# Two fused attention layers: denominators by 32x32 transposes and one product, seven split steps, and seven moved steps

## The chip, the cores and the metric

The kernel runs on one core of one Trainium2 chip. A core has five engines that run their own instruction streams side by side and wait for each other by semaphores: TensorE (PE, matrix products; its weight loads are listed as PEld), VectorE (DVE), ScalarE (ACT), GpSimd (POOL) and SyncE (SP, which here only issues DMA transfers). The metric is the device time of one execution in microseconds (us); lower is better.

## The reference

Input and output are four images of 64 x 64 positions, that is 4096 tokens, with 256 channels each. Two self-attention layers follow each other on every image (biases left out below where they are added in the plain way):

```python
# layer 1 (l = 0 in the kernel): queries and keys of 32 channels, values of 256
q, k, v = x @ Wq + bq, x @ Wk + bk, x @ Wv + bv
energy = jnp.einsum('bnd,bmd->bnm', q, k)           # 4096 x 4096 per image
x = gamma * jnp.einsum('bnm,bmc->bnc', softmax(energy), v) + x
# layer 2 (l = 1): queries g and keys f of 32 channels, values of 128
f, g, v = x @ Wf + bf, x @ Wg + bg, x @ Wh + bh
beta = softmax(jnp.einsum('bqd,bkd->bqk', g, f))
x = x + jnp.einsum('bqk,bkd->bqd', beta, v) @ Wo + bo
```

A softmax needs, for each query, the exponential of its 4096 scores and the sum of these exponentials, its denominator.

## The kernel before

The images are worked on one after the other. In each image layer 1 runs over 16 blocks of 256 queries and layer 2 over 8 blocks `j` of 512 queries. A block of layer 2 has 16 steps `i`; each step is one `Step` and covers 256 keys. Within a step TensorE makes the scores, keys on the partitions and queries along the row (L532), ScalarE takes the exponential `p` of all 128 x 1024 of them (L544), and TensorE multiplies `p` with the values and adds up in PSUM over the steps (L600). The scores of step `i + 2` are issued ahead of the products of step `i`. They go to two PSUM buffers in turn, called "st" and "pair", each of which is free again when ScalarE has read the scores that are in it.

**Two forms of a step.** A whole step multiplies `p` in fp32. A split step (every step of layer 1, in layer 2 those of `SPLIT1`) takes a second exponential `high` (L542) scaled down by a constant bias; VectorE makes `low` = p - high (L555) and `d`, a correction (L560), and TensorE runs three fp32r products, of `high`, `low` and `d`, with values that are cut in the same way. High and low of a step are issued together, d one step later. Layer 2 has six split steps and ten whole ones per block before the change. `V1` counts the whole steps, and with it go the number of value tiles, the number of early x tiles (`LEAD`) and of the start's side tiles (`LEAD_BUFS`).

**The denominators of layer 2.** All `p` of a block are added up. VectorE adds those of the "kept" steps into `p_sum` (L571, L573). The steps in `MOVED_SUMS` are added by DMA on GpSimd's queue: the `p` of the first one is copied to a tile of tag "e" (L548), that of each further one is added to it by an accumulating DMA (L550). There is one "e" tile, so each of these DMAs waits until the one before has landed. At the block's end VectorE adds the last products to `o` (L657), the moved sums to `p_sum` (L659) and both halves of `p_sum` to `sums` (L660). The four units `output(t)` run within the next block, at its steps 1 to 4: TensorE multiplies `o` by Wo (L667) and, for 128 queries at a time, `sums` by a column of ones (L668), which sums over the partitions and leaves the denominators one per partition; VectorE takes the reciprocal (L670), ScalarE scales with it (L673), and a DMA on GpSimd's queue adds `y` to the output (L675).

**Buffers.** `wide` (L267) gives 128 x 1024 tiles by tag: three of "p" (whole steps), two each of "t" (`high` and `p` of split steps) and "l" (`low` and `d`), one of "d" (`p_sum`) and one of "e". A tile is written again only when all of its readers are done, a DMA that reads it included. `small` (L510) gives four 128 x 256 tiles for layer 1's residual (x_res, x1) and layer 2's `y`.

**Order of work.** The Python loop at L735 writes one order of instructions; each engine runs its part of it strictly in that order. `plan` (L702) places smaller units of work at fixed steps: the ends of the block before at steps 1 to 4, and, for the next layer or image, units of transposes (L392 on VectorE, by 32 x 32 squares), of the q and k projection (L418 to L442, whose result goes to DRAM by L446) and of the value projection (L460). In layer 2 of the first three images these units prepare the next image; the fourth image has none. Loads of q and k (L493) and the accumulating DMAs stand on GpSimd's queue, which also runs the additions L639 and L751; x_res (L750), x1 (L632), the residual output (L640), qk_dram (L446) and the transposed loads (L280) stand on SyncE's.

**The q and k projection.** Its PSUM buffer is one of two side buffers. ScalarE copies the lower half to an SBUF tile "qk" (L439), VectorE adds the upper half and the bias to it (L440), and from that tile the upper part is cast (L441) and the rest found by a subtraction (L442).

**The end.** After the last block the kernel tests all denominators and the largest values against bounds (L807 to L822); where a bound is broken, a general path computes everything anew. It isn't taken with these inputs.

Of the kernel before, what the change touches and what calls it, by code (L numbers as in the profile page):

```python
# [50 lines left out]
F32 = mybir.dt.float32  # L51
# [16 lines left out]
SPLIT1 = (0, 3, 5, 8, 11, 13)  # L68
MOVED_SUMS = (0, 4, 7, 9, 12)
# [169 lines left out]
def fast_path(ctx: ExitStack, tc: tile.TileContext, x, w0, w1, wo, bo, gamma, out, off):  # L239
# [70 lines left out]

    inverse = const.tile([P, 2, B * N // P], F32, name="inverse")
# [12 lines left out]
    for l, (q_w, q_b, k_w, k_b, v_w, v_b) in enumerate((w0, w1)):  # L324
        queue = (nc.scalar, nc.gpsimd)[l]
        w_sb = work.tile([P, NCC, 2 * D], F32, tag="small", bufs=4, name=f"wqk_whole{l}")
# [33 lines left out]
    def bias_units():  # L360


        def issue():
            nc.vector.tensor_scalar(bv, bv, gamma_sb, None, ALU.mult)
            wide_bias = work.tile([P, P], F32, tag="small", bufs=4, name="wide_bias")
# [10 lines left out]
    q_t, moved_sums, first_p, waiting = {}, {}, [], {}  # L376
# [35 lines left out]
    def project_units(b, l, h):  # L412
# [5 lines left out]
        def qk_unit():  # L418
# [10 lines left out]
            whole = data.tile([2 * D, QB0], F32, tag="qk", name=f"qk_{b}_{l}_{h}")  # L429
# [9 lines left out]
            nc.scalar.copy(whole, ps[bottom, :])  # L439
            nc.vector.scalar_tensor_tensor(whole, ps[top, :], bqk[l], whole, ALU.add, ALU.add)  # L440
# [69 lines left out]
    def small(name):  # L510
        return work.tile([P, C], F32, tag="small", bufs=4, name=name)


    class Step:
# [8 lines left out]
        def scores(self):  # L523
# [19 lines left out]
            self.p = wide("t" if self.split and l == 1 else "p", f"p_{self.key}")  # L543
            nc.scalar.activation(self.p, s_flat, AF.Exp)  # L544
            if l == 1 and i in MOVED_SUMS:
                if i == MOVED_SUMS[0]:
                    moved_sums[b, j] = wide("e", f"p_sum_moved_{b}_{j}")
                    nc.gpsimd.dma_start(moved_sums[b, j], self.p)  # L548
                else:
                    nc.gpsimd.dma_start(moved_sums[b, j], self.p, accum_op=ALU.add)  # L550
# [13 lines left out]
        def add_up(self, p_sum):  # L564
# [3 lines left out]
            if self.i == kept[0]:  # L568
                first_p.append(self.p)
            elif self.i == kept[1]:  # L570
                nc.vector.tensor_add(p_sum, first_p.pop(0), self.p)  # L571
            else:
                nc.vector.tensor_add(p_sum, p_sum, self.p)  # L573
# [299 lines left out]
```

## Time and profile before

| | before |
|---|---|
| time, median of 3 runs | 3157.56 us (3156.2 to 3158.73) |
| the profiled execution's own time | 3155.92 us |
| its span in the trace | 3154.1 us |
| mean granted TensorE clock | 0.998 of full speed |
| busy: TensorE / VectorE / ScalarE / GpSimd | 99 / 85 / 68 / 29 % |
| accumulating DMAs of the moved sums (L550), copies (L548) | 128, 32; 512 KB each |
| L668 (denominators), L667 (output projection) | 256, 256 matmul records |

The busy time of an engine is the time in which it has at least one instruction at work, as a share of the span. Matmuls overlap each other in the pipeline, so the price of one is better read from the distance between the starts of two than from its own duration. One statement of the source, such as a fp32 product of 128 x 512, can show up as several records. For a DMA the trace has the issuing instruction on the queue's engine and the landing of the data.

### The profile page before, as it was taken

What the parts mean: (1) busy time and instruction counts of PE and PEld (TensorE: products, weight loads), DVE (VectorE), ACT (ScalarE), POOL (GpSimd) and SP (SyncE); (2) the same over time, 40 slices, a digit from 0 to 9 for tenths busy, and PEclk for the clock granted to TensorE, in tenths of its full rate; (3) what the DMA queues carried; (4) which work ended last, traced back from release to release, by engine and by line L of the source; (5) the groups of instructions that cost most, each with busy time, mean ns of one, the idle gap of its engine ahead of it and who ended that gap; (6) DMA issues with size and microseconds to landing.
All of it is one profiled execution on the core that took longest, in us unless ns stands there. A gap on an engine that the chain in (4) does not pass through costs nothing.

```text
span 3154.1 us, 54090 instructions
## 1 busy us (share of the span) xinstructions
PE 3116.3 (99%) x19908; PEld 2672.0 (85%) x19908; DVE 2689.1 (85%) x3237; ACT 2140.1 (68%) x2835; POOL 900.7 (29%) x1108
## 2 busy tenths in 40 slices
PE   8999999999999999999999999999999999999997
PEld 7999998666799999866679999976668999996664
DVE  7888888888888888888888888898888888888876
ACT  7666666777666666777766666677776666666674
POOL 5232224222422222422242222232223222233221
PEclk9999999999999999999999999999999999999999
DMA  4121114555512121555541112255554111125454
GB/s 119 43 53 47 48 48 104 107 108 105 104 44 51 41 53 47 113 101 112 107 93 47 49 45 51 51 116 107 105 113 81 48 46 47 49 65 105 97 95 73
DMA packets 391392, 239.49 MB, mean 76 GB/s; under 512 B 266672, under 2 KB 355248, under 8 KB 391120
## 3 DMA queue, kind: packets, MB, share of 16 engines
q0 software_dynamic: 68160, 134.86, 22.0%
q1 hardware_dynamic: 322048, 100.76, 13.4%
q8 instruction: 161, 2.64, 0.4%
q14 instruction: 111, 0.91, 0.1%
q10 hardware_dynamic: 912, 0.33, 0.1%
HBM read 82.58 MB, written 67.11 MB: 47 GB/s over the span
## 4 chain that ended last, share of the span: by engine, by line
PE 91%; DVE 3%; DMA 2%; issue 2%; ACT 1%; POOL 0%; SPq 0%; DVEq 0%; ACTq 0%; POOLq 0%
PE acc L600 24%; PE acc L582 23%; PE acc_pair L582 23%; PE st L532 14%; PE psv L464 4%; PE psqk L422 2%; PE pso L667 2%; DVE d L560 1%; DVE low L555 1%; ACT p L544 1%; DVE p_sum L573 1%; DMA p_sum_moved<-p 0%; DMA squares<-in_x 0%; PE pso L668 0%; DMA squares<-x_dram 0%
## 5 line engine op out<-in xcount | busy, mean ns | idle before, releaser
L542 ACT ACTIVATE high<-st,down 128x1024 fp32r<-128x1024 f32 x704 | 786.5, 1117 | 703.2 <-PE st L532 362.8
L544 ACT ACTIVATE p<-st 128x1024 f32<-128x1024 f32 x1024 | 1042.5, 1021 | 166.3 <-PE st L532 143.8
L560 DVE SCALAR_TENSOR_TENSOR d<-low,high 128x1024 fp32r<-128x1024 f32 x704 | 871.0, 1237 | 227.0 <-PE acc_pair L582 223.7
L555 DVE TENSOR_TENSOR low<-p,high 128x1024 fp32r<-128x1024 f32 x704 | 936.6, 1330 | 142.6 <-ACT p L544 141.6
L532 PE MATMUL st<-q,k 128*128 128x256 f32 (+1 forms) x3072 | 706.3, 338 | 2.5 <-DMA k<-qk_parts 1.4
L600 PE MATMUL acc<-p,v 128*128 128x512 f32 x1280 | 611.0, 597 | 0.0
L532 PEld LDWEIGHTS st<-q,k 128*128 128x128 f32 x3072 | 470.0, 189 | 103.3 <-issue 40.6
L639 POOL TENSOR_TENSOR x_res<-x,bo 128x256 f32<-128x256 f32 x128 | 212.5, 1660 | 879.3 <-DVE x L628 879.2
L600 PEld LDWEIGHTS acc<-p,v 128*128 128x128 f32 x1280 | 233.1, 189 | 161.8 <-issue 143.4
L573 DVE TENSOR_TENSOR p_sum<-p_sum,p 128x1024 f32<-128x1024 f32 x288 | 352.6, 1224 | 9.4 <-ACT p L544 5.8
L582 PE MATMUL acc<-v0h,high 128*128 128x258 f32 x2048 | 341.6, 284 | 1.2 <-ACT high L542 1.2
L582 PE MATMUL acc<-v0d,d 128*128 128x258 f32 x2048 | 339.2, 287 | 2.6 <-DVE d L560 2.2
L582 PE MATMUL acc<-v0l,low 128*128 128x256 f32 (+1 forms) x2048 | 329.3, 283 | 0.6 <-DVE low L555 0.5
L582 PE MATMUL acc_pair<-v0h,high 128*128 128x258 f32 x2048 | 329.8, 283 | 0.0
L582 PE MATMUL acc_pair<-v0l,low 128*128 128x256 f32 (+1 forms) x2048 | 328.8, 282 | 0.0
L582 PE MATMUL acc_pair<-v0d,d 128*128 128x258 f32 x2048 | 328.5, 282 | 0.0
L582 PEld LDWEIGHTS acc<-v0h,high 128*128 128x128 f32 x2048 | 286.0, 189 | 3.1 <-issue 1.4
L582 PEld LDWEIGHTS acc<-v0d,d 128*128 128x128 f32 x2048 | 281.5, 190 | 5.6 <-DVE d L560 4.9
L582 PEld LDWEIGHTS acc<-v0l,low 128*128 128x128 f32 x2048 | 282.2, 190 | 1.8 <-DVE low L555 1.3
L582 PEld LDWEIGHTS acc_pair<-v0h,high 128*128 128x128 f32 x2048 | 282.1, 189 | 0.0
L582 PEld LDWEIGHTS acc_pair<-v0l,low 128*128 128x128 f32 x2048 | 281.1, 189 | 0.0
L582 PEld LDWEIGHTS acc_pair<-v0d,d 128*128 128x128 f32 x2048 | 281.0, 189 | 0.0
(108 smaller groups left out, 3332.5 us busy)
## 6 DMA issues: line engine op xcount, KB each, us to landing
p_sum_moved<-p POOLq DMA_DIRECT2D x160, 512.0 KB, 4.7
x_res<-in_x SPq DMA_DIRECT2D x128, 128.0 KB, 2.1
qk_dram<-qk_parts SPq DMA_DIRECT2D x128, 128.0 KB, 1.9
x_dram<-x SPq DMA_DIRECT2D x128, 128.0 KB, 1.7
out<-x_res SPq DMA_DIRECT2D x128, 128.0 KB, 1.7
squares<-x_dram SPq DMA_DIRECT2D x512, 32.0 KB, 1.9
out<-y POOLq DMA_DIRECT2D x128, 128.0 KB, 3.2
q<-qk_dram POOLq DMA_DIRECT2D x252, 64.0 KB, 2.2
```

The lines of the kernel that those rows point to most:

```text
L422: nc.tensor.matmul(ps, wqk[l][:, c, :], x_parts[key][n][:, c, :], start=(c == n == 0), stop=(c == NCC - 1 and n == 1),)
L464: nc.tensor.matmul(ps[:, t, :], xT[key][:, c, t * P : (t + 1) * P], wv[l][:, c, :], start=(c == 0), stop=(c == NCC - 1),)
L532: nc.tensor.matmul(st[:, g, :], k_t[b, l, kt // NT][:, kt % NT * P : (kt % NT + 1) * P], q_t[b, l, j * n // QB][:, q0 : q0 + n], start=Tru ...
L542: nc.scalar.activation(self.high, s_flat, AF.Exp, bias=down)
L544: nc.scalar.activation(self.p, s_flat, AF.Exp)
L555: nc.vector.tensor_sub(self.low, self.p, self.high.bitcast(F32))
L560: nc.vector.scalar_tensor_tensor(self.d, self.low.bitcast(F32), -UP, self.high.bitcast(F32), ALU.mult, ALU.add)
L573: nc.vector.tensor_add(p_sum, p_sum, self.p)
L582: nc.tensor.matmul(acc[2 * s + which][:, :width], p[:, g * QB0 + s * P : g * QB0 + (s + 1) * P], v0[self.i][v][:, g, :width], start=self.f ...
L600: nc.tensor.matmul(acc[which], v_part[:, g, :], p[:, g * QB : (g + 1) * QB], start=first and g == 0, stop=last and g == G[1] - 1,)
L639: nc.gpsimd.tensor_add(x_old[s], x_new[s], bo_sb)
L667: nc.tensor.matmul(ps[:, :C], part, wo_sb, start=True, stop=True)
```

## The change

- `SPLIT1` gets seven steps instead of six, so a block of layer 2 has nine whole steps instead of ten. `V1`, `LEAD` and `LEAD_BUFS` change with it from 10, 5, 6 to 9, 4, 7.
- `MOVED_SUMS` gets seven steps instead of five. The `p` of its first step, step 2, is written by ScalarE directly to the "e" tile as the base; there is no copy any more, and the six others are added to it by accumulating DMAs. VectorE has nine steps to add instead of eleven; `p_sum` is taken from tag "d" only at the second kept step. Since step 2 is a split step, its `low` reads the base.
- The denominators: the two halves of `p_sum` are added in place. A new unit `turn` transposes the 128 x 512 sums by 32 x 32 squares on VectorE and reduces each row of 32 (128 x 16 values left). A second unit `denominators` multiplies them by the constant `same`, which holds a one wherever row and column agree modulo 32, and takes four reciprocals of 32 x 4 values. The units stand at steps 1 and 2, and the four outputs move to steps 3 to 6. The last block of the fourth image keeps the products with ones. `same` is made at the start by seven GpSimd instructions.
- At the block's end the addition of the moved sums now stands ahead of the additions to `o`.
- The q and k sum stays in its PSUM side buffer (the "qk" tile goes), so that this buffer is read until the subtraction, L442 before and L449 after. `small` has three buffers instead of four.
- The tests against the bounds are split: all but the last block's denominators are tested at step 13 of the last block, the last four columns at the end.

```diff
-SPLIT1 = (0, 3, 5, 8, 11, 13)
-MOVED_SUMS = (0, 4, 7, 9, 12)
+SPLIT1 = (0, 2, 4, 7, 9, 11, 13)
+MOVED_SUMS = (2, 3, 5, 6, 8, 10, 12)
...
+    same = const.tile([P, P], F32, name="same")
+    nc.gpsimd.tensor_copy(same[:, :S], ident[:, :S])
+    for a in range(1, P // S):
+        nc.gpsimd.tensor_add(same[:, :S], same[:, :S], ident[:, a * S : (a + 1) * S])
+    for a in range(1, P // S):
+        nc.gpsimd.tensor_copy(same[:, a * S : (a + 1) * S], same[:, :S])
     inverse = const.tile([P, 2, B * N // P], F32, name="inverse")
...
                     )
-            whole = data.tile([2 * D, QB0], F32, tag="qk", name=f"qk_{b}_{l}_{h}")
             lead = b == l == 0 and h % 2 == 1
...
             top, bottom = slice(0, 2 * D), slice(2 * D, P)
-            nc.scalar.copy(whole, ps[bottom, :])
-            nc.vector.scalar_tensor_tensor(whole, ps[top, :], bqk[l], whole, ALU.add, ALU.add)
+            whole, rest = ps[top, :], parts[top, :].bitcast(F32)
+            nc.scalar.copy(rest, ps[bottom, :])
+            nc.vector.scalar_tensor_tensor(whole, whole, bqk[l], rest, ALU.add, ALU.add)
             nc.scalar.copy(parts[top, :], whole)
...
     def small(name):
-        return work.tile([P, C], F32, tag="small", bufs=4, name=name)
+        return work.tile([P, C], F32, tag="small", bufs=3, name=name)
...
                 nc.scalar.activation(self.high, s_flat, AF.Exp, bias=down)
-            self.p = wide("t" if self.split and l == 1 else "p", f"p_{self.key}")
+            base = l == 1 and i == MOVED_SUMS[0]
+            self.p = wide("e" if base else "t" if self.split and l == 1 else "p", f"p_{self.key}")
             nc.scalar.activation(self.p, s_flat, AF.Exp)
-            if l == 1 and i in MOVED_SUMS:
-                if i == MOVED_SUMS[0]:
-                    moved_sums[b, j] = wide("e", f"p_sum_moved_{b}_{j}")
-                    nc.gpsimd.dma_start(moved_sums[b, j], self.p)
-                else:
-                    nc.gpsimd.dma_start(moved_sums[b, j], self.p, accum_op=ALU.add)
+            if base:
+                moved_sums[b, j] = self.p
+            elif l == 1 and i in MOVED_SUMS:
+                nc.gpsimd.dma_start(moved_sums[b, j], self.p, accum_op=ALU.add)
...
-        def add_up(self, p_sum):
+        def add_up(self):
             if self.l == 0 or self.i in MOVED_SUMS:
...
                 first_p.append(self.p)
-            elif self.i == kept[1]:
-                nc.vector.tensor_add(p_sum, first_p.pop(0), self.p)
-            else:
-                nc.vector.tensor_add(p_sum, p_sum, self.p)
+                return
+            so_far = first_p.pop(0) if self.i == kept[1] else p_sums[self.b, self.j]
+            if self.i == kept[1]:
+                p_sums[self.b, self.j] = wide("d", f"p_sum_{self.b}_{self.j}")
+            nc.vector.tensor_add(p_sums[self.b, self.j], so_far, self.p)
...
-    def end_second(b, j, acc, p_sum, o):
+    def end_second(b, j, acc, o):
         key = f"{b}_{j}"
+        p_sum = p_sums[b, j]
+        nc.vector.tensor_add(p_sum, p_sum, moved_sums[b, j])
         for h in range(QB // QB0):
             nc.vector.tensor_add(o[h][:, :QB0], o[h][:, :QB0], acc[1][:, h * QB0 : (h + 1) * QB0])
-        sums = work.tile([P, QB], F32, tag="sums", bufs=1, name=f"sums_{key}")
-        nc.vector.tensor_add(p_sum, p_sum, moved_sums[b, j])
-        nc.vector.tensor_add(sums, p_sum[:, :QB], p_sum[:, QB:])
+        sums, squares = p_sum[:, :QB], p_sum[:, QB:]
+        nc.vector.tensor_add(sums, sums, squares)
+        n0 = (b * N + j * QB) // P
+        end = b == B - 1 and j == NQ[1] - 1
+        part_sums = work.tile([P, QB // S], F32, tag="part_sums", bufs=1, name=f"part_sums_{key}")
+        def turn():
+            nc.vector.transpose(squares, sums)
+            nc.vector.tensor_reduce(part_sums, squares.rearrange("p (n k) -> p n k", k=S), AX.X, ALU.add)
+        def denominators():
+            ps = side_psum(f"psd_{key}")[:, : QB // S]
+            nc.tensor.matmul(ps, same, part_sums, start=True, stop=True)
+            for a in range(P // S):
+                rows = slice(a * S, (a + 1) * S)
+                of_rows = ps[rows, :].rearrange("p (t a) -> p t a", a=P // S)[:, :, a]
+                nc.vector.reciprocal(inverse[rows, 1, n0 : n0 + NT], of_rows)
...
                 nc.tensor.matmul(ps[:, :C], part, wo_sb, start=True, stop=True)
-                nc.tensor.matmul(ps[:, C : C + 1], sums[:, tok], ones[:, :1], start=True, stop=True)
-                n = (b * N + j * QB) // P + t
-                nc.vector.reciprocal(inverse[:, 1, n : n + 1], ps[:, C : C + 1])
+                n = n0 + t
+                if end:
+                    nc.tensor.matmul(ps[:, C : C + 1], sums[:, tok], ones[:, :1], start=True, stop=True)
+                    nc.vector.reciprocal(inverse[:, 1, n : n + 1], ps[:, C : C + 1])
...
-        return [output(t) for t in range(NT)]
+        return ([] if end else [turn, denominators]) + [output(t) for t in range(NT)]
...
             u()
+    size = const.tile([P, 1], F32, name="size")
+    flat = inverse.rearrange("p l n -> p (l n)")
+    before_last_block, in_last_block = flat[:, : 2 * B * N // P - NT], flat[:, 2 * B * N // P - NT :]
+    def check(values):
+        good = wide("t", f"good_{values.shape[1]}")[:, : values.shape[1]]
+        worst = work.tile([P, 1], F32, tag="g", name=f"worst_{values.shape[1]}")
+        nc.vector.tensor_scalar(good, values, 1.0 / SUM_MAX, None, ALU.is_ge)
+        nc.vector.tensor_scalar(values, values, 1.0 / SUM_MIN, None, ALU.is_le)
+        nc.vector.tensor_mul(good, good, values)
+        nc.vector.tensor_reduce(worst, good, AX.X, ALU.min)
+        nc.vector.tensor_mul(size, size, worst)
+    def check_all_but_last():
+        worst = work.tile([P, 1], F32, tag="g", name="worst")
+        nc.vector.tensor_mul(size, gamma_sb, gamma_sb)
+        nc.vector.tensor_scalar(size, size, GAMMA_MAX**2, None, ALU.is_le)
+        nc.vector.tensor_scalar(seen_v, seen_v, VALUE_MAX, None, ALU.is_le)
+        nc.vector.tensor_reduce(worst, seen_v, AX.XY, ALU.min)
+        nc.vector.tensor_mul(size, size, worst)
+        check(before_last_block)
...
                 put(1 + n, u)
+        if (b, j) == (B - 1, NQ[1] - 1):
+            put(NI[1] - 3, check_all_but_last)
         if b + 1 < B:
...
         if s.last:
-            ends = end_first(b, j, acc) if l == 0 else end_second(b, j, acc, p_sum, o)
+            ends = end_first(b, j, acc) if l == 0 else end_second(b, j, acc, o)
     run(ends)
-    good = small("good").rearrange("p (l n) -> p l n", l=2)
-    nc.vector.tensor_scalar(good, inverse, 1.0 / SUM_MAX, None, ALU.is_ge)
-    nc.vector.tensor_scalar(inverse, inverse, 1.0 / SUM_MIN, None, ALU.is_le)
-    nc.vector.tensor_mul(good, good, inverse)
-    nc.vector.tensor_scalar(seen_v, seen_v, VALUE_MAX, None, ALU.is_le)
-    size = const.tile([P, 1], F32, name="size")
-    nc.vector.tensor_mul(size, gamma_sb, gamma_sb)
-    nc.vector.tensor_scalar(size, size, GAMMA_MAX**2, None, ALU.is_le)
+    check(in_last_block)
     low = const.tile([P, 1], F32, name="low")
-    for seen, axes in ((good, AX.XY), (seen_v, AX.XY)):
-        nc.vector.tensor_reduce(low, seen, axes, ALU.min)
-        nc.vector.tensor_mul(size, size, low)
     nc.vector.tensor_scalar(low, size, 1.0, None, ALU.is_lt)
```

More of the change, by code (lines that the diff above doesn't have):

```diff
@@ L325, in fast_path @@
         queue = (nc.scalar, nc.gpsimd)[l]
-        w_sb = work.tile([P, NCC, 2 * D], F32, tag="small", bufs=4, name=f"wqk_whole{l}")
+        w_sb = work.tile([P, NCC, 2 * D], F32, tag="small", bufs=3, name=f"wqk_whole{l}")
         b_sb = const.tile([2 * D, 1], F32, name=f"bqk{l}")
@@ L364, in issue @@
             nc.vector.tensor_scalar(bv, bv, gamma_sb, None, ALU.mult)
-            wide_bias = work.tile([P, P], F32, tag="small", bufs=4, name="wide_bias")
+            wide_bias = work.tile([P, P], F32, tag="small", bufs=3, name="wide_bias")
             nc.vector.memset(wide_bias, 1.0)
@@ L375, in fast_path @@
     qk_dram, x1_dram = {}, {}
-    q_t, moved_sums, first_p, waiting = {}, {}, [], {}
+    q_t, p_sums, moved_sums, first_p, waiting = {}, {}, {}, [], {}
     def transpose_unit(b, l, h):
@@ L699, in fast_path @@
     keys = [(b, l, j) for b in range(B) for l in range(2) for j in range(NB)][NB:]
-    acc, p_sum, units = None, None, {}
+    acc, units = None, {}
     def plan(b, l, j, ends):
@@ L742, in fast_path @@
                 acc += [pair[:, a, :] for a in range(2)]
-            if l == 1:
-                p_sum = wide("d", f"p_sum_{b}_{j}")
         if l == 0 and s.last:
@@ L768, in fast_path @@
         after.cut_low()
-        s.add_up(p_sum)
+        s.add_up()
         todo = units.get(s.i, [])
```

## Prediction

> **What bounds the kernel now.** I read the page's busy shares and the chain that ended last, then the instructions in order of time for the fourth image, whose second layer prepares no next image, then the accumulating DMAs. First the page:
>
> ```profile
> PE 3116.3 (99%) x19908; PEld 2672.0 (85%) x19908; DVE 2689.1 (85%) x3237; ACT 2140.1 (68%) x2835; POOL 900.7 (29%) x1108
> PE 91%; DVE 3%; DMA 2%; issue 2%; ACT 1%; POOL 0%; SPq 0%; DVEq 0%; ACTq 0%; POOLq 0%
> ```
>
> TensorE is the bound, with almost no slack. Its prices come from distances between starts, not from the recorded (overlapping) durations. TensorE in order of time, fourth image:
>
> ```profile
> 3013.16 0.62 PE L532 MATMUL st<-q,k 128*128 128x512 f32 x2
> 3013.62 1.88 PE L600 MATMUL acc<-p,v 128*128 128x512 f32 x4
> 3014.93 1.03 PE L600 MATMUL acc<-d,v 128*128 128x512 f32 x2
> 3015.80 0.63 PE L532 MATMUL st<-q,k 128*128 128x512 f32 x2
> 3016.27 1.88 PE L600 MATMUL acc<-p,v 128*128 128x512 f32 x4
> 3017.58 1.03 PE L532 MATMUL st<-q,k 128*128 128x512 f32 x2
> 3018.45 0.63 PE L600 MATMUL acc<-high,v 128*128 128x512 f32 x2
> 3018.91 0.62 PE L600 MATMUL acc<-low,v 128*128 128x512 f32 x2
> ```
>
> A score group or a pair of high, low or d products costs 0.46 us. From 3016.27 to 3018.45 a whole step (four records of p) and a score group take 2.18, so a whole step is 1.72 and a three-product step 1.38. The denominators, second image:
>
> ```profile
> 1344.38 0.59 PE L667 MATMUL pso<-wo,o 128*128 128x256 f32 x2
> 1344.81 0.28 PE L668 MATMUL pso<-ones,sums 128*128 128x1 f32 x2
> 1344.95 0.70 PE L600 MATMUL acc<-high,v 128*128 128x512 f32 x2
> 1345.50 0.63 PE L600 MATMUL acc<-low,v 128*128 128x512 f32 x2
> ```
>
> L668 takes 0.14 and makes the next pair 0.55 instead of 0.46: 0.22 each. A block of the fourth image is then 16x0.46 + 10x1.72 + 6x1.38 + 4x0.43 + 4x0.22 = 35.4 us; the starts of L659 there lie 35.51 apart. So nothing but TensorE's work sets these blocks. GpSimd's queue in one of them:
>
> ```profile
> 2994.06 0.55 POOL L548 DMA_DIRECT2D p_sum_moved<-p  x1 [4.62 <-issue]
> ...
> 2999.61 0.89 POOL L550 DMA_DIRECT2D p_sum_moved<-p  x1
> ...
> 3007.57 0.87 POOL L550 DMA_DIRECT2D p_sum_moved<-p  x1 [1.53 <-ACT p L544]
> 3012.73 0.87 POOL L550 DMA_DIRECT2D p_sum_moved<-p  x1 [4.30 <-issue]
> 3017.80 0.87 POOL L550 DMA_DIRECT2D p_sum_moved<-p  x1 [4.20 <-ACT p L544]
> 3022.94 2.01 POOL L493 DMA_DIRECT2D q<-qk_dram  x4 [4.28 <-PE st L532]
> ```
>
> One plain copy and four accumulations into one tile: back to back they follow at 5.1 us. The tile's own view over that stretch:
>
> ```profile
> DMA to landing us min/median/max: 2.9/4.6/6.4
> ```
>
> The last one lands some 4 to 5 us before L659 needs it: today the chain is hidden.
>
> **The Trainium skill.** DMA: Bandwidth & Descriptors, "Rules for kernel authors": an accumulating DMA reads its destination and writes it later, so another one must wait for its semaphore. The trace agrees: GpSimd idles 4.2 to 4.3 us between two. Its "Anatomy of one DMA — SWDGE (gpsimd) path" gives 2.0 us plus bytes/436e3, an estimate of 3.2 us for 512 KB; measured are 2.9 for the copy and 4.6 for an accumulation, and I use the latter. TensorE: Matmul & The Clock Gate, "Architectural detail", has ScalarE and VectorE strictly first in, first out; no row here differs, and the argument rests on it. FP8 and Floating Point Precision, "TensorE Precision Notes", has four passes for true FP32; 0.86 against 0.23 us per product is 3.7.
>
> **The change, part by part.**
>
> *TensorE's work.* Per block one whole step becomes three products: -0.34. Four L668 go (-0.88, except in the last block), one 128x16 product comes; by L668's row 0.24 (bounds 0.22 and 0.35). Sum -0.98 a block, -30 in all.
>
> *VectorE and ScalarE.* VectorE: one more low and d (+2x1.14 between starts), two adds fewer (-2.28), a 128x512 transpose (0.63 between starts, 0.70 in L392's row), a reduce (128x256 takes 0.42 at L817, so 0.6 to 0.8), four reciprocals for four. +1.3 a block on 28.2 busy in 35.4: hidden under TensorE; uncovered it would cost 31x1.3 = 40. ScalarE: one more exponential, +1.0 on 24.0, also hidden.
>
> *Score buffers.* Even and odd steps use two buffers. In the changed instruction order TensorE has the scores of step 5 right behind those of step 3 in most blocks, with 0 to 0.46 us of work between; both use the same buffer, so step 5 waits for p of step 3. From rows: ScalarE starts 0.7 after a score group's start, takes 1.02, the next group 0.07 later: 1.8, of which 0.46 is the group. Stall 1.4 with nothing between, 1.2 with a projection piece between, 0.9 with 0.46, 0.25 with 1.1. In the first three images blocks 2 to 7 stall 1.4, 1.2, 0, 1.4, 1.4, 0.25. Scores of step 2 wait unread meanwhile, since ScalarE has p3 and p5 ahead of high2 and p2.
>
> *The moved sums.* This decides. Before: a copy at step 0, then four accumulations. Now p of step 2 is itself the base, and six follow (3, 5, 6, 8, 10, 12), each waiting for the one before; the first also waits until VectorE's low of step 2 has read the base. The p ring holds three, nine whole steps use it, so p of the next block's step 1 takes the buffer of step 12 and waits for the sixth landing. Behind it on ScalarE's queue stand p3, p5, high2, p2: the next chain's beginning. It is a loop. From p1's start: p1 ends 1.02, scores 3 start 1.09, p3 starts 1.8 and ends 2.8, scores 5 start 2.9, p5 starts 3.6, high2 4.5, p2 5.5 to 6.5, low2 to 7.8, first accumulation issued 8.0. Then 5x5.1 + 4.6 = 30.1, plus about 1.6 because three of the six share the DMA engines with the four y transfers (5.3 instead of 4.6): 39.7 us. VectorE's L665 waits for the same landing with the o adds and d of step 0 queued behind it, which take less than this loop.
>
> *Fourth image.* 39.7 against 35.5. Block 0: +0.8 (no y transfers, p2 right after p3: 36.4 against a block of 35.6). Block 1, same ScalarE order, 37.8: +2.3. Blocks 2 to 6: 5x4.2. Block 7, to its L665: 39.7 against 34.5, +5.2. Sum +29.
>
> *First three images.* The starts of L659 give bodies of blocks 1 to 7 in the first: 40.9, 43.4, 40.1, 38.9, 41.4, 42.2, 37.7. TensorE's share changes by -7.8 an image, the score stalls add +5.65. The loop (39 to 40.5) fits under most bodies, not under block 4 (37.9: +1.5 after some slack) nor block 7 (37.0), where GpSimd also issues the next image's k loads between accumulations: loop 43, +4.5. Sum +3.8 an image, +11.4.
>
> *Start and tail.* The qk sum now stays in its side PSUM buffer until L449: one cast (0.40) and one subtraction (0.42) longer, with TensorE already waiting 0.44 on that release in the lead: +3 (0 to 10). The seven copies and adds for `same` sit on GpSimd, which idles 4.2 us before its first k load: 0. "small" with three buffers: x1 of the second half waits for the x1 write and GpSimd's add, done 0.8 us earlier in today's rows, and x_res moves behind two DMAs on SP's queue, a block ahead of need: 0; if that cover went, 64x1. The last y waits for the first's landing (+1.8), the earlier check takes about 2.9 off the end: -1.1.
>
> Total 29 + 11.4 + 3 - 1.1 = +42.6 on the profiled execution's 3155.9 (span 3154.1), so 3198.5; the median of the runs is 1.6 higher: 3200.
>
> **Rivals.**
> A, faster: TensorE's sum decides, 3157.6 - 31 = 3126. For it: today's 99% and blocks that match the sum. Place: the step-12 landing. It decides if a link takes at most 4.4 us, so that 8.0 + six links is 34.5; against it: the measured 5.1.
> B: the chain hides, only the score stalls bite: -30.4 + 3x5.65 + 6x0.9 - 1 = -9, 3148. It needs the loop to start 4 us earlier than worked out.
> C: links of 5.9 in the first three images too, where copies for the next image share the engines (6.4 is the longest seen): 3 us more in 21 blocks, about 2 after slack: 3240.
> That the change does not do what it says is not among them: its built order has all its parts.
>
> **How the numbers follow.** Likeliest 0.70, own range 3175 to 3225; A 0.06, B 0.09, C 0.15. Range 3150 to 3235: it leaves out A, a part of B, and the upper half of C. A measurement of this kernel can tell about 0.2%, 6.3 us, from no change. Faster 0.12 (A, two thirds of B), same 0.06, slower 0.82.
>
> **What the profile after would show.** The starts of L665 in the fourth image 38 to 41 us apart; ScalarE's p and VectorE's L665 waiting for the moved-sum DMA; GpSimd idle about 4 us before each accumulation, never more for long; TensorE idle before L539. Wrong if those starts lie 34.5 to 35.5 apart, or if accumulations overlap or land within 4 us.

## The result and the profile after

The changed kernel takes 3299.81 us (median of 4 runs, 3296.1 to 3300.68) against 3158.14 us (4 runs, 3156.2 to 3160.17) for the kernel before: a ratio of 1.0446, 95% interval 1.0428 to 1.0464, so 142 us slower. The direction was forecast, the size was not: 3200 (3150 to 3235) was on record. The profiled span is 3298.8 us, 144.7 above the one before.

The page after, busy shares and the chain that ended last (the view could follow it over about a tenth of the span only):

```profile
PE 3162.7 (96%) x19786; PEld 2670.5 (81%) x19786; DVE 2725.2 (83%) x3312; ACT 2160.3 (65%) x2867; POOL 905.9 (27%) x1147
DMA 4%; issue 2%; PE 1%; ACT 1%; POOL 1%; DVE 0%; POOLq 0%; ACTq 0%
```

TensorE has lost its 99%, and where the chain can be followed it now leads through the accumulating DMAs. The waits say who waits for what (engine, line, releaser: us in total, times, longest):

```profile
POOL p L557 <- DMA p<-p: 289.7, 95, 4.8
...
ACT p L553 <- DMA p<-p: 82.0, 47, 3.1
...
PE st L539 <- ACT p L553: 50.3, 58, 3.7
...
PE st L539 <- DMA k<-qk_dram: 14.2, 4, 3.9
```

ScalarE waits 47 times for the landing of an accumulation (10 times, 10.2 us, before), and TensorE 58 times for ScalarE to free the scores (0.8 us before). Four waits are for a k load; the prediction had none.

GpSimd's queue in a block of the fourth image shows the six links (a link is one accumulating DMA of the moved sums) and the next chain's start:

```profile
3129.89 0.92 POOL L557 DMA_DIRECT2D p<-p  x1 [10.76 <-DVE inverse L686]
...
3135.16 0.86 POOL L557 DMA_DIRECT2D p<-p  x1 [1.66 <-DMA p<-p]
...
3140.33 0.86 POOL L557 DMA_DIRECT2D p<-p  x1 [2.52 <-DMA p<-p]
...
3145.63 0.87 POOL L557 DMA_DIRECT2D p<-p  x1 [3.55 <-DMA p<-p]
3150.74 0.88 POOL L557 DMA_DIRECT2D p<-p  x1 [4.24 <-DMA p<-p]
3155.80 0.87 POOL L557 DMA_DIRECT2D p<-p  x1 [4.18 <-issue]
...
3169.15 0.92 POOL L557 DMA_DIRECT2D p<-p  x1 [10.49 <-DVE inverse L686]
```

From 3129.89 to 3169.15 is a loop of 39.3 us; 39.7 was predicted. The last link lands at 3160.88. What follows is, step by step, what the prediction had written out; ScalarE:

```profile
3160.97 1.02 ACT L553 ACTIVATE p<-st 128x1024 f32<-128x1024 f32 x1 [2.11 <-DMA p<-p]
3162.81 1.03 ACT L553 ACTIVATE p<-st 128x1024 f32<-128x1024 f32 x1 [0.82 <-PE st L539]
3164.65 1.02 ACT L553 ACTIVATE p<-st 128x1024 f32<-128x1024 f32 x1 [0.81 <-PE st L539]
3165.57 1.11 ACT L549 ACTIVATE high<-st,down 128x1024 fp32r<-128x1024 f32 x1
3166.57 1.03 ACT L553 ACTIVATE p<-st 128x1024 f32<-128x1024 f32 x1
```

These are p of steps 1, 3 and 5, then high and p of step 2; low of step 2 follows at 3167.63, the first link at 3169.15, 8.3 us after the landing (8.0 predicted). The same stretch in the first image, which prepares the second one:

```profile
702.25 1.94 ACT L553 ACTIVATE p<-st 128x1024 f32<-128x1024 f32 x2 [1.82 <-DMA p<-p]
704.21 0.37 ACT L446 COPY qk_parts<-psqk 64x256 f32<-64x256 f32 x1
705.87 0.37 ACT L448 CAST qk_parts<-psqk 64x256 fp32r<-64x256 f32 x1 [1.29 <-DVE psqk L447]
706.30 0.60 ACT L487 ACTIVATE v0h<-psv 128x512 fp32r<-128x512 f32 x1
706.79 0.59 ACT L488 ACTIVATE v0l<-psv 128x512 fp32r<-128x512 f32 x1
707.27 0.20 ACT L488 ACTIVATION_READ_ACCUMULATOR v0l<-psv 128x1 f32 x1
707.69 1.02 ACT L553 ACTIVATE p<-st 128x1024 f32<-128x1024 f32 x1 [0.21 <-PE st L539]
709.96 1.12 ACT L549 ACTIVATE high<-st,down 128x1024 fp32r<-128x1024 f32 x1 [1.25 <-DVE d L567]
710.98 1.93 ACT L553 ACTIVATE p<-st 128x1024 f32<-128x1024 f32 x2
```

Between p of step 3 and p of step 5 stand four casts and copies of the next image's projections, one of them waiting for VectorE. The first link goes out at 713.75, 11.6 us after the landing at 702.16. Over blocks 1 to 6 of the first three images this part is 10.5 us in the mean and the six links take 32.3 (8.3 to 11.7, 31.2 to 34.0): a loop of 42.8. After block 0 this part is longer: 17.0 to 18.1 us in the four images.

In block 0 a load stands behind the links (first image, all engines):

```profile
564.53 0.86 POOL L557 DMA_DIRECT2D p<-p  x1 [4.19 <-ACT o L659]
565.07 2.33 POOL L500 DMA_DIRECT2D k<-qk_dram  x4
...
570.72 0.77 PE L539 MATMUL st<-q,k 128*128 128x512 f32 x1 [3.50 <-DMA k<-qk_dram]
```

The layer's last k load is behind the sixth link on GpSimd's queue, and TensorE waits 3.5 us for it, 3.1 to 3.9 in each image. TensorE's clock falls around it (from, to, length, then busy us and counts of PE, PEld, DVE, ACT, POOL, the granted clock, DMA share and GB/s):

```profile
556.00:564.00 8.00, 5.68 (x19) 2.94 (x17) 6.76 (x7) 3.96 (x6) 0.86 (x1) 0.99 0.83 153
564.00:574.00 10.00, 5.57 (x15) 4.18 (x15) 2.93 (x4) 2.56 (x3) 3.81 (x7) 0.50 0.40 79
574.00:580.00 6.00, 6.00 (x20) 3.64 (x19) 5.15 (x8) 4.74 (x8) 1.00 (x3) 0.99 0.50 88
```

The Trainium skill (TensorE: Matmul & The Clock Gate, "Part 1: The HAM clock gate (the "warmup" mystery)") has a clock that is either full or half, and half after an idle window of about 3.4 us. The trace agrees on the half, 0.50. But this stretch begins within the second of two waits of 1.6 and 1.7 us, ahead of the one of 3.5, so shorter ones were enough here: in the 3.4 us before it TensorE was idle for 2.2 us, in two pieces (matmul ends are modelled in the trace, so about). The mean clock over the span is 0.984 (0.998 before).

Where the 144.7 us came from, by starts of the first and last product of layer 1 and of the addition of the moved sums (L659, after L665), changed minus before:

| part | predicted | measured |
|---|---|---|
| layer 1 (its first product included), images 1 to 4 | +3, 0, 0, 0 | +8.6, +2.8, +2.3, -0.3 |
| second layer, block 0, images 1 to 3 | in the next line | +8.6, +8.2, +9.0 |
| blocks 1 to 7, images 1 to 3 | +3.8 each, block 0 included | +18.8, +22.1, +21.3 |
| fourth image, block 0 | +0.8 | +9.1 |
| fourth image, blocks 1 to 7 | +28.5 | +34.9 |
| tail | -1.1 | -0.8 |

### The profile page after: what moved, and what is told of

Read it like the earlier page. It is cut to its first block, busy times and chain, and to the rows that moved or that the text cites. A ratio compares the mean times of both kernels' runs of the same rounds, so it can differ in the third digit from the quotient of the medians.

```text
span 3298.8 us, 54003 instructions
## 1 busy us (share of the span) xinstructions
PE 3162.7 (96%) x19786; PEld 2670.5 (81%) x19786; DVE 2725.2 (83%) x3312; ACT 2160.3 (65%) x2867; POOL 905.9 (27%) x1147
## 5 line engine op out<-in xcount | busy, mean ns | idle before, releaser
L549 ACT ACTIVATE high<-st,down 128x1024 fp32r<-128x1024 f32 x736 | 822.2, 1117 | 714.5 <-PE st L539 346.8
L562 DVE TENSOR_TENSOR low<-p,high 128x1024 fp32r<-128x1024 f32 x736 | 962.9, 1308 | 202.5 <-ACT p L553 200.1
L567 DVE SCALAR_TENSOR_TENSOR d<-low,high 128x1024 fp32r<-128x1024 f32 x736 | 911.7, 1239 | 243.6 <-PE acc_pair L590 238.7
L539 PE MATMUL st<-q,k 128*128 128x256 f32 (+1 forms) x3072 | 726.0, 344 | 67.2 <-ACT p L553 50.3
L539 PEld LDWEIGHTS st<-q,k 128*128 128x128 f32 x3072 | 468.0, 191 | 194.0 <-ACT p L553 104.8
L608 PE MATMUL acc<-p,v 128*128 128x512 f32 x1152 | 565.1, 600 | 1.4 <-DVE o L667 1.4
L647 POOL TENSOR_TENSOR x_res<-x,bo 128x256 f32<-128x256 f32 x128 | 204.9, 1601 | 860.3 <-DVE x L636 860.1
L557 POOL DMA_DIRECT2D p<-p x192 | 169.8, 884 | 870.6 <-DMA p<-p 289.7
L608 PEld LDWEIGHTS acc<-p,v 128*128 128x128 f32 x1152 | 218.3, 192 | 128.2 <-issue 96.8
L581 DVE TENSOR_TENSOR p_sum<-p_sum,p 128x1024 f32<-128x1024 f32 x224 | 273.1, 1219 | 27.7 <-ACT p L553 25.7
```

Of the source, the lines that this page charges most:

```text
L539: nc.tensor.matmul(st[:, g, :], k_t[b, l, kt // NT][:, kt % NT * P : (kt % NT + 1) * P], q_t[b, l, j * n // QB][:, q0 : q0 + n], start=Tru ...
L549: nc.scalar.activation(self.high, s_flat, AF.Exp, bias=down)
L562: nc.vector.tensor_sub(self.low, self.p, self.high.bitcast(F32))
L567: nc.vector.scalar_tensor_tensor(self.d, self.low.bitcast(F32), -UP, self.high.bitcast(F32), ALU.mult, ALU.add)
L581: nc.vector.tensor_add(p_sums[self.b, self.j], so_far, self.p)
L608: nc.tensor.matmul(acc[which], v_part[:, g, :], p[:, g * QB : (g + 1) * QB], start=first and g == 0, stop=last and g == G[1] - 1,)
```

## The experiments

Differences are medians against the kernel before, run beside it on the same chip (its median was 3158.1 to 3162.0). Theory: the loop of six links sets the blocks. Rivals: VectorE's and ScalarE's work, the order of the scores, or the other parts of the change.

**How many links.** Three kernels differ from the changed one only in the moved steps. A step that is no longer moved is added by VectorE, so chain5 has two additions more there in each block, links5 one more and links7 one fewer:

```diff
-MOVED_SUMS = (2, 3, 5, 6, 8, 10, 12)
+MOVED_SUMS = (2, 3, 6, 8, 12)                 # chain5: four links
+MOVED_SUMS = (2, 3, 5, 6, 8, 12)              # links5: five
+MOVED_SUMS = (2, 3, 5, 6, 8, 10, 12, 14)      # links7: seven
```

> The changed kernel with five moved steps (2, 3, 6, 8, 12) instead of seven: base in place and four accumulating DMAs; VectorE adds steps 5 and 10 itself (+2.4 us a block). Theory (the loop of six accumulations sets the blocks): the loop falls by 2 x 5.1 us, from 43 to about 33 us in the first three images and from 39.2 to about 29 in the fourth, under TensorE's work there, the k load of block 0 comes two links earlier, and what is left is TensorE's -30 plus at most 22 of score stalls: 3130 to 3155 us. Rival (the time comes from VectorE's longer queue and the order of the scores): no gain, or 2.4 us a block more: 3300 to 3375.

> The changed kernel with step 10 taken out of the moved steps: five accumulating DMAs instead of six, one more addition on VectorE. Theory (above its knee the time grows by one link, 5.1 us, a block; below it what the four-link version showed stays): the loop is 38 us in the first three images and 34 in the fourth, below the 41 to 43 and 37 us of the blocks with four links, so 3235 to 3250. Rival (each link costs a share, as would be if the DMAs slowed the engines): half way between four and six links, 3267.

> The changed kernel with step 14 as an eighth moved step: seven accumulating DMAs, one addition fewer on VectorE. Theory (the loop sets the blocks): one link more, about 4 to 5.1 us in 28 to 31 blocks, +110 to +160: 3410 to 3460. Rival (the loop is not what sets the blocks with six links): under 3340.

| links | median us | ratio, 95% interval | against before |
|---|---|---|---|
| 4 | 3233.87 | 1.0231, 1.0214 to 1.0248 | +74 |
| 5 | 3250.76 | 1.0277, 1.0260 to 1.0294 | +89 |
| 6 (the change) | 3299.81 | 1.0446, 1.0428 to 1.0464 | +142 |
| 7 | 3433.68 | 1.0863, 1.0845 to 1.0881 | +272 |

The seventh link costs 130 us, 4 us in each of 32 blocks, and with it VectorE waits for the landing in every block of the fourth image:

```profile
L665 DVE TENSOR_TENSOR p_sum<-p_sum,p x8: 1225/1226/1226, 3091.0 to 3410.9; 128x1024 f32<-128x1024 f32 x8
its engine sat idle before it (us, times) until:
  DMA p<-p: 56.8, 8
```

The steps grow from 14 to 53 and 130 us, so the loop takes over around five links. So the loop is shown, but taking two links away gives back only 67 us of the 142: 74 are left, where the theory expected none. chain5 fell between both of its expectations. Its two further additions on VectorE may hide a part of what the loop costs.

**The k load.** The last k load of each second layer goes to ScalarE's queue:

```diff
-            nc.gpsimd.dma_start(dst[n * D : (n + 1) * D, :], parts[h, which])
+            if direct:   # l == 1 and j == NB - 1
+                nc.scalar.dma_start(dst[n * D : (n + 1) * D, :].bitcast(F32), parts[h, which].bitcast(F32))
+            else:
+                nc.gpsimd.dma_start(dst[n * D : (n + 1) * D, :], parts[h, which])
```

> The changed kernel with the last k load of each second layer issued on ScalarE's queue, so that it does not stand behind the accumulations of block 0. Theory (TensorE's waits of 3.1 to 3.9 us on that load in block 0, and the half-speed clock around it, cost four times 5 to 6 us): 3275 to 3285. Rival (the block is held by its chain anyway, the stall only moves on): 3295 to 3305.

Measured 3275.1 (1.0365, 1.0348 to 1.0382), 26 us of the 142 less, as expected. Block 0 was 8.2 to 9.1 us longer than before and is now 3.7 to 5.0 us longer; that is 16 us over the four images. TensorE still waits 3.7 us for the load in the fourth image, and the half-speed stretches around block 0 come to 24 us instead of 41.

**The denominators in the changed kernel.** Products with ones instead of turn, reduce and one product. This is not quite the old form: `sums` stays a half of `p_sum`, where the kernel before has a tile of its own for it.

```diff
-                if end:
+                if True:
                     nc.tensor.matmul(ps[:, C : C + 1], sums[:, tok], ones[:, :1], start=True, stop=True)
...
-        return ([] if end else [turn, denominators]) + [output(t) for t in range(NT)]
+        return [output(t) for t in range(NT)]
```

> The changed kernel with the denominators by products with ones as before, without transpose, reduce and 128x16 product. Theory (the loop of accumulations has slack for TensorE's +0.64 us a block and VectorE's transposes stand mostly beside ScalarE's queue): 3285 to 3305. Rival 1 (transpose and reduce, 1.4 us a block, stand in the loop ahead of low of step 2): 3255 to 3270. Rival 2 (TensorE's work counts in full): 3320.

Measured 3360.1 (1.0638, 1.0621 to 1.0656): 59 us slower than the change, so all three expectations fell. Two more runs looked for the reason: the outputs at steps 3 to 6 again (`put(3 + n, u)`), and products with ones with four links (`MOVED_SUMS` of chain5).

> The changed kernel with the products with ones, as in the run ones_products, but with the four outputs at steps 3 to 6 of the next block, where the change has them, and not at 1 to 4. Theory (3360 came from where TensorE meets the sums: at step 1 it stands in its queue until the last accumulation has landed and is added): 3295 to 3320. Rival (the product with ones itself is what costs): 3350 to 3365.

> The run chain5 (seven splits, four links, 3234 us) with products with ones in place of transpose, reduce and the one product. Theory 1 (the 60 us came through the loop of six links, whose beginning the products delay): without a binding loop they cost TensorE's 0.64 us a block at most and give VectorE 1.4 back: 3215 to 3255. Theory 2 (they delay every block, loop or not): 3280 to 3300.

ones_late took 3404.85 (1.0765, 1.0747 to 1.0783): the later place made it worse by 45 us, so neither expectation held. ones_four took 3296.6 (1.0439, 1.0422 to 1.0456), 63 above chain5, as the second theory had it: the loss is there with four links too. VectorE in a block of ones_four:

```profile
3115.07 0.17 DVE L697 RECIPROCAL inverse<-pso 128x1 f32<-128x1 f32 x1 [1.81 <-PE pso L696]
3115.20 1.22 DVE L562 TENSOR_TENSOR low<-p,high 128x1024 fp32r<-128x1024 f32 x1
3116.46 1.22 DVE L567 SCALAR_TENSOR_TENSOR d<-low,high 128x1024 fp32r<-128x1024 f32 x1
3117.97 0.17 DVE L697 RECIPROCAL inverse<-pso 128x1 f32<-128x1 f32 x1 [0.29 <-PE pso L696]
3119.95 1.23 DVE L581 TENSOR_TENSOR p_sum<-p,p 128x1024 f32<-128x1024 f32 x1 [1.80 <-PE pso L696]
```

and ScalarE beside it:

```profile
3117.80 1.12 ACT L549 ACTIVATE high<-st,down 128x1024 fp32r<-128x1024 f32 x1 [1.90 <-DVE d L567]
...
3121.20 1.02 ACT L553 ACTIVATE p<-st 128x1024 f32<-128x1024 f32 x1 [1.92 <-DVE p_sum L581]
```

Two things wait for TensorE here. A reciprocal does, and low and d stand behind it on VectorE. And so does the addition at 3119.95: it writes the `p_sum` of the next block, for which there is one tile, and it starts when the fourth product with ones (L696) has read the sums that are still in it. The loop in the source writes this addition ahead of these products; in the order that VectorE runs it stands behind the third reciprocal, so the loop's order is not kept there. The kernel before runs the same addition right behind its first reciprocal, and it waits for nothing:

```profile
3102.41 1.20 DVE L571 TENSOR_TENSOR p_sum<-p,p 128x1024 f32<-128x1024 f32 x1
```

From the addition of the moved sums to this one are 3.6 us in the kernel before (median of 28 blocks), 5.3 in chain5, 11.5 in ones_four and ones_products and 13.5 in ones_late. ScalarE waits for the buffers that VectorE's instructions free, and TensorE for ScalarE. In ones_four VectorE's waits at the reciprocals are 45.4 us (14.2 in the kernel before, 0.4 with the one product of chain5), its first addition waits 34.8 us for L696 (in 22 blocks), and ScalarE's p waits 46.4 us for additions (4.0 in chain5). How the 63 us divide between the waiting reciprocals and the tile that is held is not shown: no run gives `sums` a tile of its own here. ones_late, which holds the tile longest and is slowest, speaks for the tile.

**The parts on the kernel before.** First the denominators alone, then with the seven split steps too:

```diff
 # denominators_only: turn and denominators as in the change; splits, moved steps, copy, small and qk as before
 # denominators_splits: the same, and
-SPLIT1 = (0, 3, 5, 8, 11, 13)
-MOVED_SUMS = (0, 4, 7, 9, 12)
+SPLIT1 = (0, 2, 4, 7, 9, 11, 13)
+MOVED_SUMS = (0, 3, 6, 8, 12)
```

> The kernel before with the new denominators alone: six split steps, the copy and four accumulations, four small buffers as before. Theory (TensorE's work sets the blocks of the kernel before): 31 blocks x (0.88 - 0.24) = -20 us, 3138. Rival (VectorE's 1.4 us a block for transpose and reduce delay its low and d, for which TensorE waits): 3150 to 3165.

> The kernel before with the new denominators and the seven split steps; moved steps 0, 3, 6, 8, 12 with the copy at step 0, four small buffers and the qk tile as before. Against the run chain5 it differs in the base (copy at step 0, not p of step 2 in place), in small and in the qk sum. Theory 1 (VectorE and ScalarE, each with a third more split step, and the new order of the scores cost what chain5 has left, 75 us): 3215 to 3235. Theory 2 (the base in place and the small ring cost it): 3150 to 3165.

denominators_only took 3159.74 (0.9998, 0.9990 to 1.0007): no gain, where the sum of TensorE's work has 20 us. TensorE in the fourth image shows why:

```profile
3035.87 0.63 PE L539 MATMUL st<-q,k 128*128 128x512 f32 x2
3036.52 0.40 PE L680 MATMUL psd<-part_sums,same 128*128 128x16 f32 x2
3036.77 1.96 PE L607 MATMUL acc<-p,v 128*128 128x512 f32 x4
3038.17 0.79 PE L539 MATMUL st<-q,k 128*128 128x512 f32 x1
```

The scores take 0.65 instead of 0.46, so TensorE waits 0.19 for the reduced sums (in the whole run the weight load of this product waits for them 26 times, 12.2 us); the product takes 0.25 here (0.14, like one of L668, in 22 of the run's 31 blocks), and the next group 1.40 instead of 1.31. That is 0.53 of the 0.92 saved, and the starts of the block ends lie 35.43 apart instead of 35.51, so about 0.3 more is lost in other small waits, which were not followed up.

denominators_splits took 3271.02 (1.0353, 1.0335 to 1.0370), above both expectations: the seven splits with their moved steps cost 109 us here. TensorE's waits in that run, most costly first:

```profile
PE acc L607 <- ACT high L549: 45.8, 44, 1.6
PE acc L607 <- DVE low L562: 9.3, 19, 1.7
```

(Before, L600 has no such wait for high, and 1.1 us for low.) ScalarE in turn waits for VectorE's additions, which hold a split step's p: 92 us (L578 and L580), where the kernel before has 19 (L573). The splits, the moved steps and the order of the work changed together here, so this run alone doesn't part them.

**Splits against links.** Two kernels on the changed one complete a square:

```diff
-SPLIT1 = (0, 2, 4, 7, 9, 11, 13)
-MOVED_SUMS = (2, 3, 5, 6, 8, 10, 12)
+SPLIT1 = (0, 2, 5, 8, 11, 13)
+MOVED_SUMS = (2, 3, 6, 9, 12)           # six_four
+MOVED_SUMS = (2, 3, 4, 6, 7, 9, 12)     # six_six
```

> The changed kernel with six split steps (0, 2, 5, 8, 11, 13) and four links (moved steps 2, 3, 6, 9, 12; base in place). With chain5 (seven splits, four links: 3234) and the change (seven, six: 3300) it makes two sides of a square. Theory (the seventh split step costs more than its 0.34 us of TensorE: VectorE is near full in the first three images, and splits two steps apart wait for each other's buffers): 3155 to 3185. Rival (the base in place, the small ring or the qk sum in PSUM cost what chain5 has left): 3215 to 3240.

> The same with six links (moved steps 2, 3, 4, 6, 7, 9, 12): the fourth corner of the square. Theory (the loop of six links sets the blocks whatever the split steps are: 39 to 43 us): 3260 to 3300, close to the change. Rival (only both together cost: VectorE has 2.4 us a block less to do here): under 3220.

| against before, us (ratio, 95% interval) | four links | six links |
|---|---|---|
| six splits | +33 (1.0108, 1.0092 to 1.0124) | +134 (1.0425, 1.0408 to 1.0442) |
| seven splits | +74 (1.0231, 1.0214 to 1.0248) | +142 (1.0446, 1.0428 to 1.0464) |

Six links alone take nearly the whole loss, whatever the splits are. With four, the seventh split costs 42 us, where the prediction had a gain of 11 (0.34 in each of 32 blocks). They don't add up: under a loop that binds anyway, the seventh split costs 7, with intervals that overlap. By stages, in us against before:

| | six splits, four links (six_four) | seven, four (chain5) | six, six (six_six) | seven, six (the change) |
|---|---|---|---|---|
| blocks 1 to 7, images 1 to 3 together | +2.7 | +41.6 | +64.4 | +62.2 |
| blocks 1 to 7, fourth image | +2.4 | +13.7 | +26.2 | +34.9 |

In the first three images either of the two, the seventh split or the two further links, brings most of the loss by itself. Blocks 1 to 7 of the first image and of the fourth in the kernel before, in six_four and in chain5 (length, then busy us of PE, PEld, DVE and so on):

```profile
558.40:843.00 284.60, 284.04 (x1054) 189.10 (x1052) 249.65 (x304) 206.74 (x291) 82.92 (x123) 1.00 0.59 112
2885.30:3133.30 248.00, 248.00 (x866) 158.72 (x865) 197.64 (x211) 167.71 (x194) 62.84 (x83) 1.00 0.51 95
```

```profile
567.80:853.80 286.00, 282.53 (x1014) 183.49 (x1012) 261.27 (x319) 205.10 (x292) 79.25 (x116) 1.00 0.54 99
2919.30:3169.80 250.50, 249.81 (x833) 156.02 (x831) 211.31 (x228) 167.92 (x195) 59.42 (x77) 0.99 0.45 79
```

```profile
568.30:867.70 299.40, 288.85 (x1048) 187.23 (x1046) 277.75 (x334) 213.35 (x301) 79.61 (x116) 1.00 0.53 96
2951.10:3212.90 261.80, 254.16 (x846) 151.69 (x844) 227.17 (x242) 173.69 (x202) 60.01 (x77) 1.00 0.43 76
```

From six_four to chain5 VectorE gets 16 us more in both stretches, and they grow by 13 and 11. VectorE is then busy for 93% of the first one. It was at 88% there before the change; the prediction compared it with the fourth image alone (80%). A full engine isn't the whole of it: in the fourth image VectorE is busy for 87% in chain5, and the blocks grow nearly as much. Which wait carries the cost of the seventh split there was not isolated; the moved steps shifted with it.

**What six_four has left, and small terms.**

```diff
 # small_four: the change with
-        return work.tile([P, C], F32, tag="small", bufs=3, name=name)
+        return work.tile([P, C], F32, tag="small", bufs=4, name=name)
 # qk_in_psum: the kernel before with the change's
+            whole, rest = ps[top, :], parts[top, :].bitcast(F32)
 # six_four_k_queue: six_four with the edit of k_queue
```

> The changed kernel with four small buffers instead of three. If the ring costs nothing, as predicted: 3295 to 3305. If the waits of ScalarE's y for an output DMA (16 us in all) and of VectorE's x1 at the start of layer 1 count: 3275 to 3290.

> The kernel before with the qk sum left in its PSUM side buffer, nothing else. The prediction's term: +3 us (0 to 10), in layer 1 of the first image, so 3161 to 3164. Rival (the buffer is held no longer than TensorE can wait): within 2 us of before. Rival 2 (it costs each projection of 128): over 3170.

> The run six_four (3192 us) with the last k load of each second layer on ScalarE's queue. Its blocks 0 of the second layer are 3.7 to 6 us longer than before in each image, and the fourth image's block 1 4 us. Theory (most of it is TensorE's wait for that k load behind the accumulations): 3170 to 3178. Rival (it is not): 3188 to 3196.

small_four: 3293.99 (1.0426, 1.0409 to 1.0442); its interval overlaps that of the change, so the fourth buffer isn't told apart from nothing. qk_in_psum: 3166.82 (1.0026, 1.0016 to 1.0035), +5 to +11 us, and in its trace 4.2 of 7.5 us lie in layer 1 of the first image, as forecast; the rest is in block 0 of the second image (1.6) and block 1 of the fourth (1.5). six_four_k_queue: 3190.51 (1.0100, 1.0084 to 1.0117), no gain: with six splits and four links the k load was not what cost. Less the 8 of qk_in_psum, some 25 of six_four's 33 us stay open; most of them lie in block 0 of each image (+3.7 to +6.0) and the first blocks of layer 1.

**A version that beats both.** The kernel before with the new denominators, placed later than in denominators_only, `same` made in block 8 of layer 1, and the split tests:

```diff
 # denominators_only, and
-            for n, u in enumerate(ends):
-                put(1 + n, u)
+            for n, u in enumerate(ends):
+                put(1 + n + (n > 0 and len(ends) == 6), u)
...
+            if b == 0 and j == 8:
+                put(2, make_same)
...
+        if (b, j) == (B - 1, NQ[1] - 1):
+            put(NI[1] - 3, check_all_but_last)
```

> The kernel before with the new denominators at steps 1 and 3 of the next block (outputs at 4 to 7), the constant made by GpSimd only in block 8 of the first layer, and the tests split as in the change; six splits and the moved steps of before. In the run denominators_only the product cost 0.33 us and TensorE waited 0.2 for it and 0.3 more beside it, which took back nearly all of the 0.92. Theory (these waits come from when the product is placed): 8 to 15 us faster than before, 3144 to 3152. Rival (VectorE's 1.7 us a block more delay something wherever the product stands): 3155 to 3162.

It took 3152.0 us, a ratio of 0.9976, 0.9967 to 0.9985: 7 us faster than the kernel before, at the edge of the first expectation. Its three edits weren't run apart. The product takes 0.14 us in the fourth image now and isn't waited for, and still the block ends mostly lie 35.32 apart there (35.51 before): 0.2 of the 0.7 us that the sum frees arrives. Over 170 us of these blocks TensorE's weight loads wait 4.8 us for VectorE's low and d, where the kernel before has no such wait. So not TensorE's sum alone sets these blocks.

## Why the prediction was right in direction and wrong in size

- **The fourth image's loop** was right in mechanism and size: 8.0 us of ScalarE and VectorE plus 31.7 of links were predicted; 8.3 to 8.8 in four of blocks 1 to 6 (10.1 and 11.9 in the others) and 30.9 in the mean were measured. (The extra for three slower links, 3 x 0.7, makes 2.1 and not 1.6; it changes little.) Most predicted signs are there: p's waits for the moved-sum DMA, GpSimd idle about 4.2 us before a link, TensorE's waits before L539. L665's own wait is small, 1.9 us in all, and block 1 came to +9.3 instead of +2.3, because 17.0 us pass after block 0 before its first link.
- **The first three images are the step that failed**: "The loop (39 to 40.5) fits under most bodies". The loop there was taken from the fourth image, with y transfers added, but ScalarE's casts for the next image stand in its middle. The term "first accumulation issued 8.0" measured 10.5, the loop 42.8, and it fits under few bodies. Blocks 1 to 7 came to +62 us instead of +11. With six splits the six links bring +64 there by themselves. But a shorter loop alone would not have saved the forecast: with seven splits and four links +42 remain, which belongs to "hidden under TensorE" below.
- **Block 0** failed too ("no y transfers, p2 right after p3", +0.8): the k load that GpSimd issues behind six links was looked for in block 7 only. Block 0 is worth 35 us over four images; another queue for the load took 16 of them back. The other 18 stay open: six_four, in which the last k load holds TensorE in the fourth image only, has 19 there.
- **"Hidden under TensorE"** failed for VectorE and ScalarE. The square gives the seventh split +42 us with four links, where -0.34 a block was put down, and denominators_only 0 instead of -20. Both were priced as TensorE's work with free slack around. The traces show that ScalarE waits for VectorE to free a split step's buffers and that TensorE waits for VectorE's reduced sums, low and d. So "nothing but TensorE's work sets these blocks" was too strong: 35.4 us of work in blocks of 35.5 means that the other engines arrive just in time, not that they have room. That these waits make up all of the 42 us is argued.
- **The denominators' sign** was right, but not the price: against products with ones in the changed kernel they are worth 59 us, not 20. Most of that is no work of TensorE: VectorE is spared four waits for TensorE, and the one `p_sum` tile comes free sooner. In the kernel before, where `sums` has its own tile, they are worth 0.
- **The score stalls**, 22 us in the prediction's sum for B, were not run apart; in chain5 TensorE waits 22.5 us for ScalarE to free the scores (0.8 before), in the change 50.3.
- **The qk term** (+3, 0 to 10) measured 5 to 11; **small** (0) is not told from 0; the **tail** (-1.1) was -0.8.
- **Rival C** had a longer loop in the first images, but for links of 5.9; there they follow at 5.4 us (median of starts), and most of what the loop grew by is ScalarE's and VectorE's part. The rivals A and B fell: no block of the fourth image came under 38.3 us.
- **The clock** was in no case. In block 0 waits of 1.6 to 3.9 us come with stretches at half speed.

## What to carry to other kernels

When work is moved to a serial chain of DMAs, follow the chain round until it meets its own beginning, and do so in each stage with all that the engines have queued there: a few casts for another stage in the middle made a loop of 39 us one of 43, in blocks of 41. A saving on the bounding engine is worth its sum only if what it waits for arrives as early as before; give the new operand its producer's finishing time, look at who stands behind a waiting instruction on an in-order queue, and ask which tile a late reader keeps from being written again. Before filling an engine that is "hidden", take its busy share in the fullest stage, not in the one that is easiest to read.

## What the runs showed that was not expected

- A matrix product of 128x16 costs TensorE no more than one of 128x1: 0.14 us and 0.09 on the next group. In the fourth image of denominators_only, where TensorE had waited 0.19 for its operand, it took 0.25. The waits cost more than the product.
- Products with ones that read the sums where the next block's sums are due cost 63 us in a kernel of 3234 us against one product of reduced sums: VectorE waits at the reciprocals and for the tile. In the kernel before, with a tile of its own for the sums, replacing them gained nothing.
- TensorE's clock fell to 0.50 for 10 us at waits of no more than 1.7 us each, and the stretch then held the one of 3.5. The run k_queue shortened these stretches and took three of the four waits for the load away, so the clock's own share of its 26 us isn't known.
